# A selective-scan layer with a gated FFN on one Trainium2 core: A dt and B u as float32r halves, the carried state added in PSUM

## The chip, the core and the metric

The kernel runs on one core of a Trainium2 chip. Five engines take part, each with its own instruction queue that it works off in order: PE (TensorE, matrix products; the profile shows its weight loads as a row of their own, PEld), DVE (VectorE), ACT (ScalarE), POOL (GpSimd) and SP (SyncE, which here issues every DMA). Matrix products land in PSUM, which has eight banks of 2 KB per partition; everything else lives in SBUF. The metric is device time in microseconds: 2809.64 us, the median of 3 runs (2807.68 to 2811.33).

## The reference

Two sequences of 1024 tokens with 512 channels go through a selective state-space layer, a layer norm, a gated FFN with 2048 hidden units, and another layer norm. Cut to what matters (all float32; N = 128 states per channel):

```python
xn = rmsnorm(x) * norm_w
xn = xn * sigmoid((xn @ select_proj_w.T + b) * select_gate)
xp = xn @ x_proj_w.T                       # low rank 128, B 128, C 128
delta = softplus(xp[..., :128] @ dt_proj_w.T + dt_proj_b)
A = -exp(A_log)                            # 512 x 128
def step(h, inp):                          # one token
    dt, bt, ct, xt = inp
    h = exp(dt[:, :, None] * A) * h + (dt * xt)[:, :, None] * bt[:, None, :]
    return h, einsum('bdn,bn->bd', h, ct)
y = scan(step, 0, ...)
x = layernorm(x + (y + x * D_param) @ out_proj_w.T)
x = layernorm(x + (silu(x @ w_gate.T) * (x @ w_up.T)) @ w_down.T)
```

## The kernel before

The state of 512 x 128 numbers per token is never stored beyond a few tiles. The 2048 tokens are cut into 64 steps of 32 tokens. A step is worked in two halves of 256 channels, a half in eight rounds of 32 channels, so there are 1024 rounds, numbered k in the loop at line 677 (r is the round within the half, h the half). States lie on the partitions.

In a round, PE makes two things for 32 channels x 32 tokens. One is B u (tile bu, line 700): the 32 tokens are the contraction, the weights are 32 rows of B, the moving operand du is u spread over a one-hot matrix. The other is the argument A dt of the exponential for the next round (tile a, decay_mm, line 409): 32 channels are the contraction, and ddt is dt spread over a one-hot matrix. Each is done in two matmuls of 512 columns (b = 0, 1), each on its own group of 32 array rows; the four matmuls of a round use the four row groups. ACT takes the exponential of a into a_sb (line 416). DVE adds the state carried from the step before to the first token of bu (line 719) and runs one scan of 1024 elements (line 720), which restarts at each channel, since the factor of the first token is kept at zero. The result h goes back to PE for the products with C (y_round, line 433), four column groups at a time, in the rounds that ROUNDS names; y lands in one bank per step, and y_out (line 447) copies it out with ACT and sums it on POOL.

POOL spreads dt and u over the one-hot matrices, one product of 512 elements per round (diag, lines 380 and 390). The carried state needs exp(A dt) of the step's first token: dt of that token is transposed (lines 306 to 316), stored, loaded as cd by all partitions (line 346), multiplied on POOL (line 354), exponentiated on ACT (line 359) and multiplied with the last column of h (line 367).

All else on PE is written as generators that yield: pre (the projections for a block of 128 or 256 tokens), post (the output projection), ffn and silu. Its class Work hands them out: in round r at most PARTS[r] units (and saved credit) of their matmuls follow the two products and the y of that round; their other steps ("E") advance once per round. A pre goes in front of the list, ahead of ffn. B (line 260) and u (line 297) are stored from pre to a DRAM tensor and loaded per step (line 338). FFN weights are fetched through five buffers (line 514), four pieces ahead. All DMAs share SP's one queue, in the order of the program.

PSUM: two buffers of two banks for bu, two banks for a, one for y, one for all other work. So bu of round k waits for the scan of k - 2, and a of round k + 1 for the exponentials of round k.

## Time and profile before

| | |
|---|---|
| median of 3 runs | 2809.64 us (2807.68 to 2811.33) |
| profiled execution: span from first to last instruction | 2803.5 us; its page gives no other time of it |
| mean granted TensorE clock | 0.991 |
| first and last start of a scan | 42.1 and 2728.2 us |
| scan, each, and count | 2287 ns x 1024 |
| DMA | 712 issues on SP, 258.8 MB, mean 92 GB/s |

A row of a group reads: line, engine, operation, output <- inputs, shape, count, then busy time in us and mean ns of one, then idle time of the engine just before and what ended it. A timeline row reads: start in us, length in us, engine, line, operation, output <- inputs, count of merged instructions, and in brackets idle time before it and what ended that. SPq is SP's queue issuing DMAs. An f32 matmul shows as two records. The length of a matmul record includes the way through the array, so records of one batch overlap; the pace is the difference of starts.

### The profile page before, as it was taken

How to read it: one execution, taken by the hardware profiler on the slowest of the kernel's cores; microseconds unless marked ns; L12 is line 12 of the kernel's file. 1: busy time of each engine (PE TensorE's matmuls, PEld its weight loads, DVE VectorE, ACT ScalarE, POOL GpSimd, SP SyncE). 2: the span in 40 equal slices, each digit the busy share in tenths (PEclk: the TensorE clock that was granted, in tenths of full speed). 3: DMA queues.
4: the chain of work that ended last, by engine and by line, in shares of the span. 5: the costliest groups of instructions: out<-in, count | busy, mean ns of one | idle time of the engine just before them, and what ended most of it. 6: DMA issues, size and time to landing. Idle time of an engine off the chain costs nothing.

```text
span 2803.5 us, 59499 instructions
## 1 busy us (share of the span) xinstructions
PE 2688.0 (96%) x23744; PEld 1476.3 (53%) x23744; DVE 2514.2 (90%) x2144; ACT 1549.9 (55%) x3105; POOL 1782.9 (64%) x2016
## 2 busy tenths in 40 slices
PE   6879999999999999999999999999999999999998
PEld 4325545555555554555545555455555555555557
DVE  3999999899999999999999999999999999999980
ACT  4546656645565455655656556565566555555542
POOL 5556666666667576765666657567575666667553
PEclk8999999999999999999999999999999999999999
DMA  2001322423223231233312333132331333332335
GB/s 76 20 27 54 108 80 70 115 82 123 65 83 113 86 125 50 89 103 109 118 56 87 98 115 113 55 93 95 114 95 60 110 97 108 100 109 93 109 99 188
DMA packets 112388, 258.80 MB, mean 92 GB/s; under 512 B 11568, under 2 KB 49456, under 8 KB 112112
## 3 DMA queue, kind: packets, MB, share of 16 engines
q1 hardware_dynamic: 112112, 254.99, 28.3%
q8 instruction: 189, 3.10, 0.5%
q14 instruction: 87, 0.71, 0.1%
HBM read 242.23 MB, written 12.71 MB: 91 GB/s over the span
## 4 chain that ended last, share of the span: by engine, by line
PE 74%; DVE 17%; issue 3%; ACT 3%; POOL 2%; DMA 1%; SPq 0%; DVEq 0%; POOLq 0%; ACTq 0%
PE bu L700 28%; PE gu L540 17%; DVE h L720 15%; PE y L433 12%; PE d L560 8%; PE a L409 3%; ACT a_sb L416 1%; PE sel L187 1%; PE op L481 1%; PE xp L187 1%; DVE bu L719 1%; DMA ub_d<-uT 1%; PE b L251 1%; PE ss L204 1%; SPq L297 0%
## 5 line engine op out<-in xcount | busy, mean ns | idle before, releaser
L720 DVE TENSOR_TENSOR_SCAN h<-a_sb,bu 128x1024 f32<-128x1024 f32 x1024 | 2340.5, 2287 | 154.8 <-PE bu L700 43.5
L416 ACT ACTIVATE a_sb<-a 128x496 f32<-128x496 f32 x2048 | 1089.9, 585 | 1109.0 <-PE a L409 1036.0
L700 PE MATMUL bu<-du,ub 32*128 32x512 f32 x4096 | 1184.3, 643 | 52.8 <-DVE h L720 31.4
L409 PE MATMUL a<-ddt,a_t 32*128 32x512 f32 x4096 | 1209.0, 643 | 2.8 <-ACT t L315 2.8
L380 POOL TENSOR_TENSOR ddt<-dt,hot 128x512 f32<-128x512 f32 x512 | 534.5, 1049 | 193.3 <-PE a L409 193.2
L540 PEld LDWEIGHTS gu<-x1T,w 128*128 128x128 f32 x4096 | 481.2, 192 | 223.7 <-issue 137.3
L390 POOL TENSOR_TENSOR du<-ub,hot 128x512 f32<-128x512 f32 x512 | 535.9, 1051 | 21.8 <-PE a L409 18.5
L540 PE MATMUL gu<-x1T,w 128*128 128x128 f32 x4096 | 535.5, 283 | 6.9 <-ACT t L315 3.5
L433 PE MATMUL y<-h,cz 128*32 128x256 f32 x9208 | 525.1, 361 | 3.0 <-ACT yc L447 1.9
L700 PEld LDWEIGHTS bu<-du,ub 32*128 32x128 f32 x4096 | 329.2, 184 | 352.4 <-issue 190.2
L433 PEld LDWEIGHTS y<-h,cz 128*32 128x32 f32 x9208 | 255.7, 109 | 405.7 <-issue 267.8
L409 PEld LDWEIGHTS a<-ddt,a_t 32*128 32x128 f32 x4096 | 347.9, 184 | 15.9 <-ACT a_sb L416 9.2
L560 PE MATMUL d<-w,hid 128*128 128x256 f32 x1024 | 257.8, 393 | 0.7 <-ACT dt L276 0.3
L578 POOL TENSOR_SCALAR gu<-gu 128x256 f32<-128x256 f32 x128 | 108.4, 847 | 223.4 <-ACT gu L548 222.9
L560 PEld LDWEIGHTS d<-w,hid 128*128 128x128 f32 x1024 | 183.2, 189 | 124.0 <-issue 91.4
L719 DVE TENSOR_TENSOR bu<-bu,cd 128x32 f32<-128x32 f32 x992 | 182.5, 184 | 65.5 <-PE a L409 61.5
L448 POOL TENSOR_TENSOR yc<-yc,pick 128x512 f32<-128x512 f32 x64 | 66.7, 1042 | 195.3 <-ACT yc L447 195.3
L586 POOL TENSOR_TENSOR hid<-gu,e 128x256 f32<-128x256 f32 x128 | 93.1, 727 | 106.1 <-ACT e L584 104.9
L367 POOL TENSOR_TENSOR cd<-cd,h 128x256 f32<-128x256 f32 x124 | 106.4, 858 | 50.2 <-DVE h L720 50.2
L579 POOL TENSOR_TENSOR gu<-gu 128x256 f32<-128x256 f32 x128 | 93.4, 730 | 10.7
L548 ACT COPY gu<-gu 128x512 f32<-128x512 f32 x128 | 75.4, 589 | 33.5 <-PE gu L540 33.4
L325 POOL TENSOR_TENSOR dt<-dt,u 128x512 f32<-128x512 f32 (+1 forms) x36 | 41.4, 1151 | 64.7 <-ACT dt L322 64.7
(86 smaller groups left out, 1243.5 us busy)
## 6 DMA issues: line engine op xcount, KB each, us to landing
w<-in_wgu_s_dram SPq DMA_DIRECT2D x256, 512.0 KB, 3.7
w<-in_wd_s_dram SPq DMA_DIRECT2D x128, 512.0 KB, 3.6
cd<-dt_d SPq DMA_DIRECT2D x62, 256.0 KB, 4.1
ub<-ub_d SPq DMA_DIRECT2D x64, 128.0 KB, 2.0
ub_d<-bt SPq DMA_DIRECT2D x64, 64.0 KB, 1.8
ub_d<-uT SPq DMA_DIRECT2D x64, 64.0 KB, 1.8
zT<-in_x_q_dram SPq DMA_DIRECT2D x16, 256.0 KB, 3.9
x<-in_x_dram SPq DMA_DIRECT2D x16, 256.0 KB, 3.7
```

The lines of the kernel that those rows point to most:

```text
L367: nc.gpsimd.tensor_tensor(cd, cd, last, ALU.mult)
L380: nc.gpsimd.tensor_tensor(ddts[j][:, m, :, :], made[lot_of[st]][0][:, a + m, toks(st)].unsqueeze(1).to_broadcast([P, 16, S]), hot[:, ts(i, ...
L390: nc.gpsimd.tensor_tensor(dus[j][:, m, :, :], uv[:, a + m, :].unsqueeze(2).to_broadcast([P, 16, S]), hot.unsqueeze(1).to_broadcast([P, 16, ...
L409: nc.tensor.matmul(ps, a_t[ts(g, 32), m, :], ddts[k // 4][ts(g, 32), m % 2, :, :], start=True, stop=True,)
L416: nc.scalar.activation(a_sb[:, k % 3, ts(b, 16), 1:], ps[:, :, 1:], AF.Exp, scale=-1.0)
L433: nc.tensor.matmul(ys[st][ts(m, 32), 256 * i + 4 * q0 : 256 * i + 4 * (q0 + nq)], cz[st % 3][:, at : at + 32], hs[h][:, 64 * m + q0 : 64 * ...
L540: nc.tensor.matmul(ps[:, ts(2 * a + b, P)], w[:, a, k, :], x1T[:, k, :], start=(k == 0), stop=(k == NM - 1),)
L560: nc.tensor.matmul(ps[:, 0:HD], hid[:, f, :], w[:, f % 4, :], start=(f == 0), stop=(f == NF - 1),)
L578: nc.gpsimd.tensor_scalar_max(g, g, -80.0)
L700: nc.tensor.matmul(bu[:, ts(b, 16), :], prepared[st][ts(g, 32), 1, :], dus[k // 4][ts(g, 32), m % 2, :, :], start=True, stop=True,)
L719: nc.vector.tensor_tensor(first, first, left[:, at : at + 2, i, :], ALU.add)
L720: nc.vector.tensor_tensor_scan(hs[h][:, ts(r, 32), :].rearrange("p q t -> p (q t)"), a_sb[:, k % 3, :, :].rearrange("p q t -> p (q t)"), b ...
```

## The change

B, u and dt are written as sums of two numbers: a high half rounded to float32r (on ACT, or by a copy to a tile of that type) and the remainder as low half. For A = exp(A_log), laid out by the host in a new order with each row four times, the two halves are built on the chip. The contraction of 32 rows in a row group now holds 8 tokens (for B u) or 8 channels (for A dt) times the four products of high and low halves; sums over 32 tokens become four matmuls of 128 columns (o = 0 to 3), and 16 channels by 32 tokens of A dt become two of 256 columns (e = 0, 1). All have float32r operands.

The carried state is no longer added by DVE. The last column of h is gathered by ACT (gather), transposed on PE into a spare half of the y bank (carry_mm), copied out, multiplied with exp(A dt) of the first token (carry) and added into bu by one more f32 matmul of 16 columns in the same PSUM accumulation (state_mm).

The y bank is now per half; the products of C with h of the half before fall in rounds 1, 2 and 3. h is split into two tiles per half with three buffers in all. The B, u and dt halves go to three DRAM tensors in smaller pieces and are loaded by nine DMAs per step. The transposition of the first dt is gone.

```diff
-ROUNDS = ((), (0, 1, 2), (), (), (3, 4, 5.0), (), (), (5.5, 6, 7))
-PARTS = (4, 0, 3, 3, 0, 3, 3, 0)
+ROUNDS = ((), (0, 1, 2), (3, 4, 5), (6, 7), (), (), (), ())
+PARTS = (3, 0, 0, 0, 3, 4, 4, 3)
...
-    dt0_d = dram.tile([NS, D], FP, name="dt0_d")
-
-    ub_d = dram.tile([NS, 4, S, 2, P], FP, name="ub_d")
+    dt_d = dram.tile([NS, 2, P, NM, S], FP, name="dt_d")
+    u_d = dram.tile([NS, 2, 4, 8, 4, P], FP, name="u_d")
+    b_d = dram.tile([NS, 8, 2, 2, 4, N], FP, name="b_d")
...
+    a_raw = half_pool.tile([P, P, S], FP, tag="h", name="a_raw", bufs=3)
+    a_raw = a_raw.rearrange("p q t -> p (q t)")
+    half_n = 4 * NM * N
+    nc.sync.dma_start(a_raw[:, 0:half_n], a_log_r)
     nc.sync.dma_start(a_t, a_log)
-    nc.sync.dma_start(a_n, a_log_t)
...
-        for t in (a_t, a_n):
-            nc.scalar.activation(t, t, AF.Exp)
+        whole, round_ = a_raw[:, 0:half_n], a_raw[:, half_n:]
+        nc.scalar.activation(whole, whole, AF.Exp)
+        nc.scalar.copy(round_.bitcast(FR), whole)
+        nc.scalar.activation(a_t, a_t, AF.Exp)
+        nc.vector.tensor_scalar_mul(whole, whole, is_lo)
+        nc.vector.scalar_tensor_tensor(
+            a_r.rearrange("p x n -> p (x n)"), round_, sign, whole, ALU.mult, ALU.add
+        )
...
+        nc.scalar.copy(bh, ps[:, 0:n].rearrange("p (j n) -> p j n", n=N))
+        yield "E"
+        bl = bt.bitcast(FR)
+        nc.gpsimd.tensor_tensor(bl, bt, bh, ALU.subtract)
         for st in range(n_s):
-            rows = bt[ts(st % 4, S), st // 4, :]
-            nc.sync.dma_start(
-                ub_d[t0 // S + st, :, :, 1, :].rearrange("g t n -> t g n"),
-                rows.unsqueeze(1).to_broadcast([S, 4, N]),
-            )
+            for c1, piece in enumerate((bh, bl)):
+                first = S * (st % 4)
+                rows = piece.bitcast(FP)[first : first + S, st // 4, :]
+                for o in range(4):
+                    nc.sync.dma_start(
+                        b_d[t0 // S + st, :, c1, :, o, :],
+                        rows[ts(o, 8), :].unsqueeze(1).to_broadcast([8, 2, N]),
+                    )
...
+        for st in range(n_s):
+            for c2, piece in enumerate((dth, dtl)):
+                nc.sync.dma_start(dt_d[t0 // S + st, c2], piece.bitcast(FP)[:, :, ts(st, S)])
...
             for st in range(4):
-                nc.sync.dma_start(
-                    ub_d[t0 // S + 4 * j + st, :, :, 0, :].rearrange("g t q -> t g q"),
-                    t[ts(st, S), :].rearrange("t (g q) -> t g q", g=4),
-                )
+                for c2, piece in enumerate((th, tl)):
+                    rows = piece.bitcast(FP)[ts(st, S), :].rearrange("t (g q) -> t g q", g=4)
+                    for o in range(4):
+                        nc.sync.dma_start(
+                            u_d[t0 // S + 4 * j + st, c2, :, :, o, :].rearrange("g t q -> t g q"),
+                            rows[ts(o, 8), :, :],
+                        )
...
+        for c in range(4):
+            nc.sync.dma_start(
+                dt_r.rearrange("(r c) e s m t -> c r (e s m t)", c=4)[c],
+                dt_d[st, c % 2].rearrange("(r x) m t -> r (x m t)", x=4),
+            )
+            nc.sync.dma_start(
+                u_r.rearrange("(r c) o q -> c r (o q)", c=4)[c],
+                u_d[st, c % 2].rearrange("g t o q -> (g t) (o q)"),
+            )
+        nc.sync.dma_start(
+            b_r.rearrange("p o n -> p (o n)"),
+            b_d[st].rearrange("t a b o n -> (t a b) (o n)").unsqueeze(0).to_broadcast([4, S, 4 * N]),
+        )
...
+    def gather(h):
+
+        lasts[h] = half_pool.tile([P, 2, P], FP, tag="last", name=f"last_{h}", bufs=1)
+        for mm in range(2):
+            nc.scalar.copy(
+                lasts[h][:, mm, :].rearrange("p (q s) -> p s q", s=2),
+                hs[h][mm][:, :, S - 1].rearrange("p (s q) -> p s q", s=2),
+            )
+
+    def carry_mm(h):
+
+        for mm in range(2):
+            nc.tensor.matmul(
+                ys[h][:, 1 - h % 2, ts(mm, N)], lasts[h][:, mm, :], ident,
+                start=True, stop=True, skip_group_check=True,
+            )
+
+    def carry(h):
...
+        nc.scalar.copy(cT.rearrange("p m n -> p (m n)"), ys[h][:, 1 - i, :])
+        yield "E"
+        for mm in range(2):
+            m = 2 * i + mm
+            nc.scalar.activation(a0[:, mm, :], a_t[:, m, :], AF.Exp, scale=nd0[:, m : m + 1])
+        yield "E"
+        nc.gpsimd.tensor_tensor(cT, cT, a0, ALU.mult)
...
-        nc.tensor.matmul(
-            ps, a_t[ts(g, 32), m, :], ddts[k // 4][ts(g, 32), m % 2, :, :],
-            start=True, stop=True,
-        )
+        for e in range(2):
+            nc.tensor.matmul(
+                ps.rearrange("p (d e) t -> p e d t", e=2)[:, e],
+                a_r[ts(g, 32), 4 * m + 2 * e + s, :], ddts[k // 4][ts(g, 32), s, e, :, :],
+                start=True, stop=True, skip_group_check=True,
+            )
...
+    def state_mm(k, b, bu):
+
+        h, mm, s, pair = place(k)
+        st, g = h // 2, 2 * pair + b
+        last = st % NSB == 0
+        for o in range(4):
+            nc.tensor.matmul(
+                bu[:, ts(b, 16), ts(o, 8)], prepared[st][1][ts(g, 32), o, :],
+                dus[k // 4][ts(g, 32), s, o, :, :],
+                start=(o == 0), stop=last and o == 3, skip_group_check=True,
+            )
+        if not last:
+            nc.tensor.matmul(
+                bu[:, ts(b, 16), 0], products[h][ts(g, 32), mm, :],
+                hot[ts(g, 32), :].rearrange("p (e s) -> p s e", s=2)[:, s, :],
+                start=False, stop=True, skip_group_check=True,
+            )
...
+            if h in products:
+                work.finish(carries.pop(h))
...
+        if r == 4 and h:
+            y_out(h - 1)
+            if h - 1 in lasts:
+                carries[h + 1] = work.add(carry(h - 1), front=True)
+        if r == 1 and h and h + 1 < 2 * NS and (h + 1) // 2 % NSB:
+            gather(h - 1)
         work.others()
...
-        if st % NSB:
-            left = carried[st].rearrange("p (b i e) -> p b i e", i=2, e=16)
-            first = bu[:, :, 0].rearrange("p (b e) -> p b e", e=16)
-            at = 4 * m + 2 * pair
-            nc.vector.tensor_tensor(first, first, left[:, at : at + 2, i, :], ALU.add)
...
+            if r == 3 and h - 1 in lasts:
+                carry_mm(h - 1)
```

## The prediction

> **What bounds the kernel now.** I read the page first: shares, the chain that ended last (PE 74%, DVE 17%), and the costliest groups.
>
> ```profile
> PE 2688.0 (96%) x23744; PEld 1476.3 (53%) x23744; DVE 2514.2 (90%) x2144; ACT 1549.9 (55%) x3105; POOL 1782.9 (64%) x2016
> ...
> L720 DVE TENSOR_TENSOR_SCAN h<-a_sb,bu 128x1024 f32<-128x1024 f32 x1024 | 2340.5, 2287 | 154.8 <-PE bu L700 43.5
> ...
> L719 DVE TENSOR_TENSOR bu<-bu,cd 128x32 f32<-128x32 f32 x992 | 182.5, 184 | 65.5 <-PE a L409 61.5
> ```
>
> PE and DVE are both nearly full. The tile view of h puts scan starts from 42.1 to 2728.2: 2686.1 / 1023 = 2.626 us a round, with 42 before the first and 73 after the last (2803.5 - 2730.5). The timeline of the first scans, which have no add before them, and of a stretch in which PE has little else give the DVE's own pace:
>
> ```profile
> 54.68 26.25 DVE L720 TENSOR_TENSOR_SCAN h<-a_sb,bu 128x1024 f32<-128x1024 f32 x12 [2.03 <-PE a L409]
> ...
> 201.32 2.29 DVE L720 TENSOR_TENSOR_SCAN h<-a_sb,bu 128x1024 f32<-128x1024 f32 x1
> 203.52 0.18 DVE L719 TENSOR_TENSOR bu<-bu,cd 128x32 f32<-128x32 f32 x1
> 203.80 2.29 DVE L720 TENSOR_TENSOR_SCAN h<-a_sb,bu 128x1024 f32<-128x1024 f32 x1
> ```
>
> With the add a round is at least 2.48; without it (26.25 - 2.29) / 11 = 2.18. Next, the four matmuls of one round, and what follows them on PE:
>
> ```profile
> 1312.74 0.69 PE L700 MATMUL bu<-du,ub 32*128 32x512 f32 x1
> 1312.75 0.69 PE L409 MATMUL a<-ddt,a_t 32*128 32x512 f32 x1
> 1312.76 0.69 PE L700 MATMUL bu<-du,ub 32*128 32x512 f32 x1
> 1312.76 0.69 PE L409 MATMUL a<-ddt,a_t 32*128 32x512 f32 x1
> ...
> 1313.81 0.38 PE L540 MATMUL gu<-x1T,w 128*128 128x128 f32 x1
> ...
> 1326.32 2.05 PE L540 MATMUL gu<-x1T,w 128*128 128x128 f32 x16
> 1328.30 0.69 PE L700 MATMUL bu<-du,ub 32*128 32x512 f32 x1
> ```
>
> An f32 matmul is two records. The four matmuls use the four row groups and run side by side; the burst lasts 1.07 (1312.74 to 1313.81). Sixteen gu records last 2.05 and eight 1.16 elsewhere, so a record of 128 columns costs 0.111; and from the first of sixteen to the next burst it takes 1.98 (1326.32 to 1328.30), so each switch costs about 0.2.
>
> PE per half (eight rounds): bursts 8 x 1.07 = 8.56; y in three batches, 1.43 (83.10 to 84.53) + 2 x 1.22 (1017.22 to 1018.44) = 3.87; the other work in units of some four 128-column records, 0.446 each. Units by the counts: gu 1024, d 512, op 128, sel 144, xp 72, some 175 more; less about 160 before the first and after the last scan: 1895 / 128 = 14.8 a half = 6.6, and five switches = 1.0. Sum 20.0, or 2.50 a round. The other 0.12 up to 2.626 is rounds where PE has less than the DVE's 2.48.
>
> **The change part by part.**
>
> *DVE.* The 992 adds go. Floor 2.18 a round; PE decides then.
>
> *The burst (B u, A dt, carry).* Per row group, bu now has four float32r matmuls of 128 columns with four weight loads, and the carried state one f32 matmul of 16 columns (two records, two loads); a has two of 256 columns. No row shows float32r. Lower end: half an f32 record per matmul, a quarter of what f32 costs at the same size: 4 x 0.056 + 2 x 0.111 + 0.2 = 0.65. Upper end: each costs what an f32 matmul of its size costs, two records: 4 x 0.223 + 0.22 + 0.2 = 1.31. I take one record of 0.111 per matmul: the operands come already split, so I assume one record instead of two, and that its 128-column weight load keeps the pace of the f32 rows. Six records and a switch: 6 x 0.111 + 0.2 = 0.87; the a groups, two records of at most 0.22 + 0.2, finish inside. Break-even is computed below.
>
> This needs groups to run past each other. The cold bursts speak for it:
>
> ```profile
> 42.60 1.22 PE L409 MATMUL a<-ddt,a_t 32*128 32x512 f32 x1
> 42.61 1.22 PE L700 MATMUL bu<-du,ub 32*128 32x512 f32 x1
> 43.08 1.59 PE L409 MATMUL a<-ddt,a_t 32*128 32x512 f32 x2
> ```
>
> The timeline of PE alone is shown. The bu matmul at 42.61 comes later in the program than both records of a at 42.60, and the second of those starts after it (a cold record of a streams until about 43.4, and the row of two at 43.08 ends at 44.67). One waiting record was passed; up to eleven weight loads and matmuls must be passed now, which no row shows. The Trainium skill ("TensorE: Matmul & The Clock Gate", Part 3, what overlaps and what doesn't) says matmuls start and end strictly in program order, which speaks against the change; these rows contradict it at a depth of one. By it the sum would be that of the serial rival below.
>
> *Other PE work per half.* y without its split matmul: 2 x 1.43 + (2 x 0.427 + 0.2) = 3.91; the transposes of the carried state, 4 records x 0.111 = 0.45; units and switches as before, 7.5 (the nine t0 batches, under 10 us in all, go). Sum 11.9, or 1.49 a round. PE round: 1.49 + 0.87 = 2.36. PE stands 0.18 above the DVE floor where it stood 0.02 above, so I allow half the old unevenness: 2.42. Loop: 1024 x 2.42 = 2478, against 2688.
>
> *ACT.* Out: cd exps 39.5 and t copies 5. In, by nearest rows: gather and exp of the first decay, some 248 each of 128 columns at 0.31 (154); cT copies 124 x 0.37 (46); y_out in two parts (+10); high copies about 20. Net +185, 62% busy. They are issued behind the round's two a_sb exps (1.06), so a round has at worst about 2.8 of ACT; a_sb has three buffers, and PE waits for a bank of a if ACT is late. At most 0.05 a round; it is in the 0.06.
>
> *POOL.* Out: cd products 78.9 + 106.4. In: 124 carry products x 0.73 = 91, the low halves and the negated first dt about 50, constants 2. Net -43. The 1024 one-hot products keep 512 elements (1.05); if writing float32r cost the 1.27 of a product without broadcast, +225 would leave POOL under 80%: nothing. The carry product at round 5 waits for ACT; ddt behind it is due four rounds later. The carry chain itself ends at round 5 and is used at round 0: some 7 us of cover.
>
> *SP.* It issues every DMA here. Its timeline at a block of 256 tokens:
>
> ```profile
> 490.80 3.75 SPq L260 DMA_DIRECT2D ub_d<-bt  x8
> ...
> 495.57 16.28 SPq L514 DMA_DIRECT2D w<-in_wgu_s_dram  x4
> ```
>
> A store costs 0.44 to 0.47 of issue (eight in 3.75; in the start four in 1.78). Per 32 tokens: 8 for B, 2 for dt, 8 for u and 9 loads, 27 issues instead of 4, about 12 us of a 39 us step: bandwidth of the queue suffices. But they come in bunches. Start: 32 + 8 + 32 stores instead of 9 are in series with the first load: +63 x 0.44 = 28, and 1 for POOL's new constants; the other new work (1 MB of a_raw, exps, low halves) lies beside it. First scan at 71. (At the 0.30 of the shortest stores, +19.) In the loop a block of 256 tokens stores 64 for B in one bunch, 28 us, and then 16 (7 us) and twice 32 (14 us each). The weight fetches queue behind. Two f-pairs of weights are in stock at the bunch (495.57 waits for free buffers), worth 5 us of z and 16 units, 23 us; the next arrives after 28 + 0.3 + 3.7 = 32. So about 9 late, less at 0.30 an issue; the later bunches some 3 each. PE stops in order and the bursts with it. I take 10 for each of the six blocks that run beside FFN: 60. Bounds: 0, and 210 (35 each, if every bunch is exposed by half). The Trainium skill ("DMA: Bandwidth & Descriptors", issuing engines are not separate DMA queues) calls issue time usually small beside the transfer. Here 0.44 stands beside 1.8 of landing, and 64 in a row are not small. By the rule this term and most of the +29 would be nothing, 2600.
>
> **Sum.** 71 + 2478 + 60 + 73 = 2682 of span, against 2803.5. The page gives no other time for that execution; the median of the runs is 6.1 above its span, so 2688. A change within 0.2% (about 6 us) could not be told from none.
>
> Break-even: (2803.5 - 71 - 60 - 73) / 1024 = 2.54 a round, less 0.05 and 1.49: a burst of 1.00. Against 1.07 today the forecast has little room.
>
> **Rivals.**
> 1. *float32r at f32's price* for these sizes, or a window too shallow, so that a and the second bu group start late: burst 1.31, round 2.80 + 0.03; 2898 + 204 + 6 = 3108, slower. For: no row shows either. Against: the halves that an f32 matmul's second record seems to be for are already rows of the contraction. It decides from a burst of 1.00.
> 2. *Strict order*: sixteen records one after another, 16 x 0.111 + 0.2 = 1.98, round 3.49: 3574 + 204 + 6 = 3784. Against: 42.61 above.
> 3. *The SP queue*: burst as forecast, but bunches starve FFN's weights by 35 a block: +150, 2838, slower. For: 28 us against 23 of stock. Against: prefetch refills between bunches.
> 4. *Loads half as long*: burst 0.65, PE 2.14, so DVE's 2.18 + 0.1 decides: 2335 + 204 + 6 = 2545.
>
> **How the numbers follow.** Forecast 0.42, rival 4 0.11, rival 1 0.27, rival 2 0.06, rival 3 0.14. Forecast alone: 2600 to 2790. Faster takes forecast and rival 4, less 0.01: 0.52; same 0.03, from the edges of forecast and rival 3; slower 0.45. The range 2560 to 3130 leaves out half of rival 4, rival 2, and the upper part of rival 1: less than 0.2.
>
> **What would show it.** Right: burst to next batch near 0.87, scans 2.18 apart where PE has little, no L719, first scan near 71. Wrong: second bu group's first record about 0.6 after the first group's (strict order); records of 128 columns 0.22 apart (price); FFN's matmuls waiting for w, with SP in stores (queue). ACT over 75% or POOL as releaser of bursts would upset the covers.

## The result, and the profile after

The changed kernel takes 3237.31 us (median of 4 runs, 3234.2 to 3243.81), against 2809.05 us for the kernel before in the same comparison: a ratio of 1.153, 95% interval 1.1515 to 1.1547. The forecast was 2688 us, faster, with a range up to 3130. Sign and range were both wrong.

The page of the changed kernel: its shares, the clock granted to TensorE in forty slices of the span (tenths of full speed, 9 is 90% or more), and the groups that answer to those of before (columns: busy us, mean ns of one | idle us just before and what ended it):

```profile
PE 2875.3 (89%) x31216; PEld 2338.6 (72%) x31216; DVE 2377.6 (74%) x1155; ACT 1731.4 (54%) x3753; POOL 1768.9 (55%) x2011
...
PEclk6679799899988998889997999979989799897898
...
L797 DVE TENSOR_TENSOR_SCAN h<-a_sb,bu 128x1024 f32<-128x1024 f32 x1024 | 2320.7, 2282 | 755.1 <-PE bu L489 671.2
...
L483 PE MATMUL bu<-du,b_r 32*128 32x128 f32 x8192 | 1032.9, 297 | 55.2 <-DVE h L797 36.7
L470 PE MATMUL a<-ddt,a_r 32*128 32x256 f32 x4096 | 853.9, 344 | 35.4 <-POOL ddt L440 28.9
```

DVE fell from 90% to 74%. Its scans now wait 671 us for the last matmul of the burst, the carry at line 489. POOL and ACT are far from full, as forecast. 8192 records for 8192 float32r matmuls of bu, and 4096 for a, say that a float32r matmul is one record. The tile view of h gives the start and the end of the loop:

```profile
L797 DVE TENSOR_TENSOR_SCAN h<-a_sb,bu x1024: 2258/2287/2291, 69.2 to 3158.8; 128x1024 f32<-128x1024 f32 x171
```

First scan at 69.2 us (forecast 71), and 71 us behind the last scan's end (3232.4 less 3161.1; forecast 73). So the whole miss lies in the loop: 3089.6 us between first and last scan start, against 2538 forecast (2478 and 60 of stalls). Three things are in it.

**The burst.** The timeline of PE in one round of the changed kernel (start us, length us, columns of the shape, count of merged records):

```profile
1307.42 0.55 PE L483 MATMUL bu<-du,b_r 32*128 32x128 f32 x3
1307.70 0.38 PE L470 MATMUL a<-ddt,a_r 32*128 32x256 f32 x1
1307.71 0.43 PE L483 MATMUL bu<-du,b_r 32*128 32x128 f32 x3
1307.92 0.23 PE L489 MATMUL bu<-hot,cT 32*128 32x16 f32 x1
1307.93 0.27 PE L470 MATMUL a<-ddt,a_r 32*128 32x256 f32 x1
...
1308.29 0.26 PE L489 MATMUL bu<-hot,cT 32*128 32x16 f32 x1
1308.47 0.71 PE L273 MATMUL b<-xp_w,xT 128*128 128x128 f32 x4
```

1307.42 to 1308.47 is 1.05 us; the median burst is 1.056, against 1.07 before and 0.87 forecast. The first row group's records follow each other by 0.11 us, as forecast (0.16 after the first; medians over the loop). But the first A dt matmul, for a free row group, starts only at 1307.70 and the second B u group at 1307.71, 0.29 us late.

The first step of a sequence has no carried state, so its rounds have the same order without the carry's matmuls. There, in most bursts, all four row groups start within 0.03 us, and this burst lasts 0.60:

```profile
94.88 0.32 PE L483 MATMUL bu<-du,b_r 32*128 32x128 f32 x1
94.89 0.38 PE L470 MATMUL a<-ddt,a_r 32*128 32x256 f32 x1
94.89 0.32 PE L483 MATMUL bu<-du,b_r 32*128 32x128 f32 x1
94.91 0.38 PE L470 MATMUL a<-ddt,a_r 32*128 32x256 f32 x1
```

So PE goes past a row group in which three B u still wait. With the two records of the carry behind them five wait, and the next group starts only when the third B u has started and three are left (B u at 0, 0.164 and 0.275 us, A dt at 0.282, medians).

**The stores.** The waits of PE, then of ACT, in the changed kernel (us in total, times, longest):

```profile
PE gu L621 <- ACT uTh L335: 100.6, 7, 15.6
PE gu L621 <- DMA w<-in_wgu_s_dram: 74.9, 10, 11.3
```

```profile
ACT uT L335 <- DMA u_d<-uT: 101.7, 7, 16.3
```

Rounds (from one scan start to the next) of over 7 us exist 16 times, and exceed 2.7 us each by 215 us in sum (forecast 60, bound 210). Some 75 us are the forecast's mechanism: FFN's matmuls stand and wait for w, which stands on SP behind 64 stores of B:

```profile
1311.24 1.32 SPq L290 DMA_DIRECT2D b_d<-bh  x4
1312.65 1.29 SPq L290 DMA_DIRECT2D b_d<-bt  x4
...
1332.47 1.33 SPq L290 DMA_DIRECT2D b_d<-bt  x4
...
1339.79 0.47 SPq L595 DMA_DIRECT2D w<-in_wgu_s_dram  x1
```

A store issues in 0.3 us, less than the 0.44 taken, and the bunch lasts 22.6 us (1311.24 to 1333.8). The other 100 were not foreseen: the copy of the second 128 tokens of u (line 335) waits up to 16.3 us on ACT until the first 128 tokens' 32 stores have left the one row buffer, and behind it on ACT stand the exps and copies that PE waits for.

**The clock.** The records of TensorE's clock hold full and half clock and nothing between. The mean is 0.890 where it was 0.991, so half clock lasted 2 x 0.110 x 3232 = 711 us (the clock's own records sum to 715; before 51). The forecast had no term for it. Windows of the changed kernel (span, length, then busy us of PE, PEld, DVE, ACT, POOL, with counts, then granted clock, DMA share, GB/s):

```profile
1995.00:1998.00 3.00, 0.61 (x14) 0.51 (x10) 2.90 (x4) 1.44 (x4) 1.11 (x2) 0.94 0.24 79
1998.00:2008.00 10.00, 10.00 (x89) 6.47 (x90) 6.58 (x3) 4.49 (x8) 2.32 (x3) 0.51 0.52 177
2008.00:2015.00 7.00, 6.93 (x85) 5.59 (x82) 5.20 (x3) 6.55 (x16) 2.39 (x4) 1.00 0.42 166
```

A gap of 2.4 us in PE's work, and then ten microseconds in which PE is busy without a pause at half clock. The kernel before, in a stretch with 14 gaps of over 0.8 us (the longest 1.44), keeps its clock:

```profile
120.00:200.00 80.00, 60.12 (x564) 22.77 (x560) 76.12 (x65) 37.03 (x71) 45.24 (x50) 0.98 0.07 20
```

Counted over the loop: before, PE has 35 gaps of 0.8 to 2.4 us, and 6 of them are followed by over 1 us of half clock in the next 6 us. In the changed kernel it has 48, and 47 are. The lengths differ, though: 31 of the 35 are under 1.5 us (4 of them followed by half clock), and 30 of the 48 (29 followed); from 1.5 to 2.4 us it is 2 of 4, and 18 of 18. The changed kernel also has 20 gaps of over 2.4 us, before none.

By rounds, the changed kernel has 864 with the clock held, at 2.706 us on average, and 159 that spend over 0.3 of their length at half clock, 751 us together (4.73 each). Against the forecast's 2.42, the first cost 864 x 0.286 = 247, of which the burst is 864 x 0.186 = 161; the others cost 751 - 159 x 2.42 - 60 = 306. Together 553, and the miss of the time is 549 (3237.3 less 2688).

The 306 are not all the clock's. The 16 rounds of over 7 us are all among the 159, and exceed the 60 that were forecast by 155. The other 143 are 106 us longer than rounds at the same place in the half with the clock held: that, as an estimate, is what the half clock costs beside the stalls.

### The profile page after: what moved, and what is told of

The parts are those of the page before. It is cut to its first block, busy times and chain, and to the rows that moved or that the text cites. A ratio compares the mean times of both kernels' runs of the same rounds, so it can differ in the third digit from the quotient of the medians.

```text
span 3232.4 us, 76245 instructions
## 1 busy us (share of the span) xinstructions
PE 2875.3 (89%) x31216; PEld 2338.6 (72%) x31216; DVE 2377.6 (74%) x1155; ACT 1731.4 (54%) x3753; POOL 1768.9 (55%) x2011
## 5 line engine op out<-in xcount | busy, mean ns | idle before, releaser
L483 PEld LDWEIGHTS bu<-du,b_r 32*128 32x128 f32 x8192 | 883.7, 198 | 323.1 <-issue 202.5
L483 PE MATMUL bu<-du,b_r 32*128 32x128 f32 x8192 | 1032.9, 297 | 55.2 <-DVE h L797 36.7
L470 PE MATMUL a<-ddt,a_r 32*128 32x256 f32 x4096 | 853.9, 344 | 35.4 <-POOL ddt L440 28.9
L440 POOL TENSOR_TENSOR ddt<-dt_r,hot 128x512 fp32r<-128x512 f32 x512 | 533.8, 1051 | 341.7 <-PE bu L489 197.8
L489 PE MATMUL bu<-hot,cT 32*128 32x16 f32 x3968 | 657.8, 251 | 0.0
L470 PEld LDWEIGHTS a<-ddt,a_r 32*128 32x128 f32 x4096 | 627.3, 195 | 39.1 <-POOL ddt L440 29.3
L489 PEld LDWEIGHTS bu<-hot,cT 32*128 32x128 f32 x3968 | 621.9, 199 | 0.0
L449 POOL TENSOR_TENSOR du<-u_r,hot 128x512 fp32r<-128x512 f32 x512 | 556.9, 1103 | 9.6 <-PE bu L483 9.4
L428 POOL TENSOR_TENSOR cT<-cT,a 128x256 f32<-128x256 f32 x124 | 90.5, 730 | 128.8 <-ACT a L426 128.8
L409 PEld LDWEIGHTS y<-ident,last 128*128 128x128 f32 x496 | 65.0, 191 | 51.5 <-issue 51.5
```

The costliest lines, as they stand in the source:

```text
L409: nc.tensor.matmul(ys[h][:, 1 - h % 2, ts(mm, N)], lasts[h][:, mm, :], ident, start=True, stop=True, skip_group_check=True,)
L440: nc.gpsimd.tensor_tensor(ddts[j][:, s, :, :, :], dt_r[:, :, s, m, :].unsqueeze(2).to_broadcast([P, 2, 8, S]), hot8.unsqueeze(1).unsqueeze ...
L449: nc.gpsimd.tensor_tensor(dus[j][:, s, :, :, :], u_r.rearrange("p o (m e s) -> p o m e s", m=NM, s=2)[:, :, m, :, s] .unsqueeze(3).to_broa ...
L470: nc.tensor.matmul(ps.rearrange("p (d e) t -> p e d t", e=2)[:, e], a_r[ts(g, 32), 4 * m + 2 * e + s, :], ddts[k // 4][ts(g, 32), s, e, :, :],
L483: nc.tensor.matmul(bu[:, ts(b, 16), ts(o, 8)], prepared[st][1][ts(g, 32), o, :], dus[k // 4][ts(g, 32), s, o, :, :], start=(o == 0), stop= ...
L489: nc.tensor.matmul(bu[:, ts(b, 16), 0], products[h][ts(g, 32), mm, :], hot[ts(g, 32), :].rearrange("p (e s) -> p s e", s=2)[:, s, :], star ...
```

## The experiments

Each time is compared with the kernel before on the same chip (2808.7 to 2813.5 us). "Half clock" is read from the clock's records of the profiled run. The order, the portions, both, and before without the add were run once each, the last table's two float32r kernels with the carry four times, all others twice.

### Order of the burst, and stores in portions

The theory: PE passes only some three waiting matmuls, so the order of the burst sets its length; and the bunches of stores make the long stalls. Three runs: the order alone, the portions alone, both. The order deals the matmuls of the four row groups out in turn; the portions are extra "E" yields in pre.

```diff
-        for b in range(2):
-            state_mm(k, b, bu)
-            if k + 1 < NG:
-                nxt.append(decay_mm(k + 1, b))
+        states = [state_mm(k, b, bu) for b in range(2)]
+        args = [decay_mm(k + 1, b) for b in range(2)] if k + 1 < NG else []
+        for gens in (states, states, args, args, states, args, states, states):
+            for gen in gens:
+                made_now = next(gen, None)
...
                         rows[ts(o, 8), :].unsqueeze(1).to_broadcast([8, 2, N]),
                     )
+            if c > 1:
+                yield "E"
```

> Only the order of a round's matmuls on TensorE changes: the four row groups take turns instead of one group's five matmuls standing first. Theory (TensorE looks only some three matmuls ahead, so the second group of B u starts 0.29 us late): the burst falls from 1.055 to 6 x 0.11 + 0.2 = 0.87 us, 1024 x 0.19 = 190 us less, about 3050 us. Rival (weight loads or the float32r stream are what fills the burst, whatever the order): burst still 1.05 us, 3237 us.

> The stores of B, dt and u of a block are handed to SP in portions of 4 or 8, one portion per round, instead of 64, 16 and 32 at once; their number stays. Theory (bunches on SP hold up the FFN's weights and the buffer of the transposed u): the stretches of 15 to 20 us without a scan, 214 us in all beyond normal rounds, go, and with them most of the half-clock time that follows them: 3237 - 214 - 60 = about 2960 us. Rival (the stalls are only where PE waits anyway, or the number of issues is what counts): within 50 us of 3237.

> Both of the changes of e1_order and e2_spread. If the two causes are separate the gains add: about 2770 us, burst 0.87 us, no gap between scans above 8 us. If the bunches and the burst hide each other, clearly more than the sum of the parts, 2900 us or more.

Order: 3054.1 us, burst 0.770. Nothing was taken away, and the burst lost 0.286 and the time 183, of 1023 x 0.286 = 293: some rounds are held by DVE now (2.20 us at two places of the half), and the stalls grew from 215 to 251 us, half clock from 715 to some 740. The timeline of PE with the order dealt out:

```profile
1300.70 0.33 PE L483 MATMUL bu<-du,b_r 32*128 32x128 f32 x2
1300.71 0.38 PE L471 MATMUL a<-ddt,a_r 32*128 32x256 f32 x2
1300.86 0.27 PE L483 MATMUL bu<-du,b_r 32*128 32x128 f32 x2
1300.93 0.28 PE L471 MATMUL a<-ddt,a_r 32*128 32x256 f32 x2
1300.97 0.39 PE L483 MATMUL bu<-du,b_r 32*128 32x128 f32 x4
1301.20 0.34 PE L489 MATMUL bu<-hot,cT 32*128 32x16 f32 x4
1301.47 0.71 PE L621 MATMUL gu<-x1T,w 128*128 128x128 f32 x4
```

All four groups start within 0.01 us, where 0.29 lay between the first and the others. No group puts more than two records in a row into the queue before the others have their turn. That the order sets the burst is thereby shown. That the limit is three waiting records of one row group, and not three in all, is read from the orders: without a carry the changed kernel passes three in each of two groups, and the float32 run of the last table starts all four groups within 0.03 us while seven records wait, at most three of one group. No run varied the number alone.

Portions: 3168.2 us, where some 2960 was expected. Of the 16 long rounds two remain, with 51 us of excess, nearly all of it in one round of 48.9 us, which was 20.3 before the portions (the third block's preparation has four steps only). Half clock stayed at 680 us. Both: 2987.5 us, half clock 704. The two gains add (183 and 69, together 250); 2770 was missed because the portions brought 69 us where 277 were expected. So most of the long stalls went (68 us are left in the run of both) and the half clock did not, which the theory of long stalls could not explain.

### Before, without the add on DVE

Line 719 of the kernel before is left out; the state of the step before is then not added.

> The kernel before with the addition of the carried state to bu on VectorE left out (the state is then not carried from step to step; the work that makes it stays). It prices that half of the change by itself. Theory (before, two thirds of the rounds last VectorE's 2.48 us while TensorE has 2.50 on average): the round falls from 2.63 to about 2.53, 2710 us. Rival (TensorE alone sets the round): 2810 us. Floor if TensorE did not matter: 2.18 a round, 2350 us.

2783.9 us, 26 less. The rival's figure of no gain is nearer. The page of this run has PE at

```profile
PE 2714.1 (98%) x23744; PEld 1497.2 (54%) x23744; DVE 2369.0 (85%) x1152; ACT 1549.2 (56%) x3105; POOL 1780.4 (64%) x2016
```

so the add was in PE's shadow almost everywhere: removing it pays little unless PE's round gets shorter too.

### What the clock follows

Four runs on the version with both edits (portions from the fourth block on): that version itself, one with a filling matmul in the rounds that have no unit of other work, one with the same matmul on 32 rows only, one with more filling.

```diff
+        if idle:
+            nc.tensor.matmul(
+                bu[:, 0:16, :].rearrange("p q t -> p (q t)"), ident, out_w[:, 0, :],
+                start=True, stop=True, skip_group_check=True,
+            )
...
+        idle = PARTS[r] and done == 0
```

> The changed kernel with the burst's matmuls dealt out in turn and the stores given in portions, as in the run of both, but the portions only from the fourth block of tokens on (the third block's preparation has too few steps to wait for portions: it left a gap of 49.9 us at round 112). Expected: 2987.5 less about 46, 2940 us; half clock for about 690 us, as before, since the burst streams as little as it did. Rival: the half clock follows from the long gaps alone, and with the last of them gone it falls below 300 us and the time below 2850.

> As the run above, and in front of the burst of each round that has no unit of other TensorE work though it may have one (83 of 1024), one plain float32 matmul of 128x128 by 128x512 into the PSUM bank that the burst then overwrites: it computes nothing that is used, and adds about 0.85 us of full-array streaming to a round of 2.2 to 2.4 us (from the 0.251 us that a float32 record of 256 columns takes in the down projection). Theory (the clock follows the share of the array's column slots that stream): the filled rounds go from a share of 0.10 to 0.45, half clock falls from 690 to 300-450 us, and the time to 2790-2860. Rival (the clock was lost to something else, the filler is only added work): half clock stays within 60 us of the run above, and the time is equal or up to 70 us longer (83 x 0.85).

> As the filled run, but the filling matmul uses 32 rows of the array instead of 128, with the same 512 columns: TensorE is busy just as long, and a quarter of the array streams. Theory of the streaming share: the filled rounds only reach 0.19, and half clock stays within 80 us of the run with no filling (about 690), the time at 2930-2990. Rival (TensorE's busy time sets the clock, whatever part of the array is used): half clock and time fall as in the full-array filling, to within 30 us of that run.

> As the full-array filling, and also a float32 matmul of 256 columns (some 0.43 us) ahead of each burst that follows the rounds 1 and 2 of a half, which hold the y products but no unit of other work; their share goes from about 0.39 to 0.57, and TensorE's work in them from 1.4 to 1.85 us, still under the scan's 2.18. Theory: half clock falls by a further 50-150 us and the time by 20-80 from the other filled run. Rival (those rounds kept their clock anyway, and TensorE is on the path there too): half clock the same, time 0-50 us longer.

| run | time us | ratio to before, 95% | half clock us |
|---|---|---|---|
| both edits | 2958.9 | 1.0495 to 1.0588 | 677 |
| filled, whole array | 2955.5 | 1.0475 to 1.0584 | 581 |
| filled, 32 rows | 2992.7 | 1.0542 to 1.0782 | 725 |
| more filling | 3054.9 | 1.0829 to 1.0938 | 486 |

The whole-array filling takes 96 us of half clock away, and the same columns on 32 rows take none. The mean clock of the second execution of each gives nearly the same: 656 us without filling, 554 with it, 667 on 32 rows, 470 with more. That speaks for the share of the array that streams, and against PE's busy time. But the size fits neither text: 581 lies between the theory's 300 to 450 and the rival's 617 and more. The filling was also expected to bring some 100 us of time and brought none, and more filling costs 96: in the rounds after 1 and 2 PE had less room than the 1.4 of 2.18 us put down for it. Against the filling on 32 rows, which adds as much work, the whole-array one has 144 us less half clock and 37 us less time (the two executions of each lie 9 and 27 us apart): by this estimate half clock costs time, but about a quarter of its length and not half. The waits of PE that the filling leaves are for DVE, w, POOL and ACT, and there no filling stands. In the version itself, with the gap of 49.9 us gone, the time fell by 29 of the 46 us expected, and half clock stayed at 677 us: the longest gaps alone do not bring it.

The same question without added work: float32r alone, put into the kernel before; and plain float32 in place of float32r in the version with both edits.

```diff
-                ddts[j] = half_pool.tile(shape, FP, tag="ddt", name=f"ddt_{j}")
+                ddts[j] = half_pool.tile(shape, FR, tag="ddt", name=f"ddt_{j}")
...
-            ps, a_t[ts(g, 32), m, :], ddts[k // 4][ts(g, 32), m % 2, :, :],
+            ps, a_tr[ts(g, 32), m, :], ddts[k // 4][ts(g, 32), m % 2, :, :],
...
-                bu[:, ts(b, 16), :], prepared[st][ts(g, 32), 1, :],
+                bu[:, ts(b, 16), :], prepared[st].bitcast(FR)[ts(g, 32), 1, :],
```

> The kernel before with one thing of the change alone: the matmuls of the burst take float32r operands (A, dt, B, u rounded once, no low halves: the products are less exact), four of 512 columns, no split, no carry matmuls, no stores added, the same order of work. Expected of the burst: 1.07 to about 0.5 us (two row groups side by side, each 2 x 512 columns at one cycle: 0.43, and a weight load). With the clock held the round would fall from 2.63 to 2.35-2.40 (scan 2.18 and the add), the time to 2500-2560. Theory (a burst that streams a quarter as much lets the clock drop where a gap comes): half clock rises from 51 to 250-600 us and takes back part of the gain: 2560-2750. Rival (the clock loss of the changed kernel comes from its stores and waits, not from float32r): half clock below 100 us, 2500-2560.

> The changed kernel in the order dealt out in turn and with the stores in portions (2958.9 us), its burst's matmuls reading the same tiles as plain float32: same split, same stores, same waits for transfers and POOL, four times the columns' cycles. Expected: burst 0.77 to 1.5-1.8 us (two row groups side by side, each 1024 columns at four cycles: 1.7), median round 3.2-3.6, time 3350-3750. Theory of the streaming share: with the burst streaming 0.85 us of full array again, half clock falls from 677 to below 200 us though the time is longer. Rival (the gaps alone bring the half clock): half clock stays above 400 us.

Float32r alone in before: 2720.4 us (ratio 0.9645 to 0.9701), burst 0.438, half clock 362 us against 51, with no store and no matmul added. The same stretch of the start that kept 0.98 of the clock before, in this run:

```profile
120.00:200.00 80.00, 51.50 (x432) 22.34 (x430) 76.70 (x65) 37.88 (x72) 43.74 (x48) 0.66 0.10 27
```

Plain float32 in the changed order: 3149.4 us (ratio 1.1115 to 1.1282), half clock 236 against 677 with the same stores, loads and order, though the run is 190 us longer. 236 lies between the theory's 200 and the rival's 400, and the time is below the 3350 to 3750 expected. The burst is 1.220, not 1.5 to 1.8: the expectation let two row groups run side by side, and there are four. The same program shows two things in its two number types. With the longer burst PE has fewer gaps of 0.8 to 2.4 us, 46 against 89. And the short ones lose the clock less often: of those under 1.5 us 11 of 34 are followed by half clock in float32, 52 of 63 in float32r. From 1.5 us on there is no such difference: 11 of 12, and 23 of 26. With float32r alone it is 40 of 109 and 40 of 51. So gaps bring the half clock on, the short ones mostly where the burst streams little. How much of the 441 us is owed to fewer gaps, and how much to the streaming, was not parted. The granted clock of the plain float32 run in forty slices, from its page, to be held against the changed kernel's row above:

```profile
PEclk6989989999999999999999999999999999999998
```

The Trainium skill ("TensorE: Matmul & The Clock Gate", Part 1, what's actually happening) says that a free-running window of some 3.4 us decides, by how busy PE has been. The stretches of half clock here are indeed 3.4 us or multiples of it; but 1998 to 2008 shows PE 10.00 of 10 us busy at 0.51, so busy in the profile's sense is not what decides. An estimate of the streaming itself: a float32 record of 256 columns in the down projection takes 0.216 us from start to start, 0.84 ns a column; a float32r record is taken at half of that (assumed), and each record is weighted with the part of the array's rows and columns that it uses. By it, the 3.4-us windows of the changed kernel before a fall have at most some 0.37 of the array streaming, median 0.19, and those that keep full clock a median of about 0.6 (before: about 0.8). The lowest of those are no higher than the highest before a fall, and before, windows of 0.26 kept full clock, so no threshold follows.

### Loads of w from ACT, and no carry

> As the 2958.9 us kernel, with the feed-forward weights' loads issued from ScalarE's queue in place of SyncE's, so that they no longer stand behind the stores and the row loads. Theory: TensorE's waits for w (59 us in 14 gaps over 1.2 us) go, with the half clock that follows them (92 us, of which half is lost): 2850-2910. Rival (an issue costs ScalarE as much as SyncE, 0.35 us x 384 = 134 us, and it lies between the exps of a round): no faster than 2950, up to 3080.

```diff
-                nc.sync.dma_start(pieces[i], sources[i])
+                nc.scalar.dma_start(pieces[i], sources[i])
```

2953.7 us (ratio 1.037 to 1.0635): no difference that can be told from 2958.9. The largest of PE's waits in this run shows what came instead:

```profile
PE a L477 <- ACT a_sb L502: 56.5, 46, 5.6
```

PE's wait for w, 44.5 us with the loads on SP, is gone from the head of the list, and the burst's wait for the exponentials, 22.0 us there, is 56.5. The loads are now issued on the queue of the exps, as the rival said, and there was no gain.

> As the 2958.9 us kernel, with the carried state left out altogether (no gather, no transpose, no exp of the carry, no carry matmul in the burst; the state starts at zero in every half, so the output lacks the carried part). Burst expected 0.77 to 0.55 (two matmuls of two records fewer). If TensorE sets the rounds with units (five of eight): 5/8 x 1023 x 0.22 = 140 us less, 2800-2840. Rival (what TensorE gains turns into gaps at half clock): 2880-2950, half clock over 720 us.

```diff
-        last = st % NSB == 0
+        last = True
...
-        if r == 1 and h and h + 1 < 2 * NS and (h + 1) // 2 % NSB:
-            gather(h - 1)
```

2765.0 us (0.9799 to 0.9865), 194 less than with the carry, where 140 was expected, and level with before or a little under it. Burst 0.592, so 0.178 less a round, 182 us if every round had it. Half clock is 609 us. So with order and portions mended, the carry costs more than the 149 us that are left between 2958.9 and before.

### Which part costs: the change without its split

The changed kernel, with one A dt and one B u matmul of 512 columns per row group and before's stores and loads, first with float32r operands rounded once, then in plain float32, then with float32r and another order of the burst.

```diff
-        for e in range(2):
-            nc.tensor.matmul(
-                ps.rearrange("p (d e) t -> p e d t", e=2)[:, e],
-                a_r[ts(g, 32), 4 * m + 2 * e + s, :], ddts[k // 4][ts(g, 32), s, e, :, :],
-                start=True, stop=True, skip_group_check=True,
-            )
+        nc.tensor.matmul(
+            ps, a_r[ts(g, 32), m, :], ddts[k // 4][ts(g, 32), s, :, :],
+            start=True, stop=True, skip_group_check=True,
+        )
...
-        for o in range(4):
-            nc.tensor.matmul(
-                bu[:, ts(b, 16), ts(o, 8)], prepared[st][1][ts(g, 32), o, :],
-                dus[k // 4][ts(g, 32), s, o, :, :],
-                start=(o == 0), stop=last and o == 3, skip_group_check=True,
-            )
+        nc.tensor.matmul(
+            bu[:, ts(b, 16), :], prepared[st].bitcast(FR)[ts(g, 32), 1, :],
+            dus[k // 4][ts(g, 32), s, :, :],
+            start=True, stop=last, skip_group_check=True,
+        )
```

> The changed kernel without its split: float32r operands rounded once (no low halves, the products are less exact), one A dt matmul and one B u matmul of 512 columns per row group as before, before's stores and one row load a step, and all the rest of the change: the order of channels, the carried state transposed and added in PSUM, C h early. If the split (its 12 more matmuls a round, its stores and row loads) is what costs, burst 0.6-0.7 us (0.44 in the run of before with float32r, and two small matmuls of two records), rounds with units 2.4-2.6, the others at the scan's 2.18, half clock 300-500 us: 2560-2720, below the 2720 of before with float32r alone. Rival (the carry's chain or the early C h costs as well: gaps of TensorE stay): 2750-2900.

> As the run above with plain float32 throughout, so the carry in PSUM and the early C h alone: the kernel before with only the second and third part of the change. Burst expected 1.07 plus 0.1 to 0.2 for the carry, and no add on VectorE. Theory (TensorE set the rounds of before, so that the add removed is worth 1% and the carry's matmuls cost more than that): 2850-3000, half clock below 100 us. Rival (the carry's matmuls fit into idle time, the add's removal is a gain): 2700-2800.

> As the first of these three, with the burst's matmuls in the order both B u, both A dt, both carries, so that neither carry stands in front of a group that is free. Theory (TensorE passes only about three waiting matmuls): burst 0.1-0.15 us shorter than in the first, in the five rounds of eight with units on the path: 30-90 us less time. Rival (six matmuls are within the look-ahead, or VectorE sets the rounds by now): within 15 us of the first.

| kernel | time us | ratio to before, 95% | burst us | half clock us |
|---|---|---|---|---|
| before | 2809.7 | 1 | 1.071 | 51 |
| carry in PSUM and early C h alone, float32 | 3065.5 | 1.0891 to 1.0935 | 1.198 | 182 |
| float32r alone | 2720.4 | 0.9645 to 0.9701 | 0.438 | 362 |
| float32r, carry in PSUM, early C h | 2641.1 | 0.9381 to 0.9417 | 0.566 | 380 |
| the same, carries last in the burst | 2616.0 | 0.9300 to 0.9330 | 0.557 | 370 |
| the change (with the split) | 3237.3 | 1.1515 to 1.1547 | 1.056 | 715 |

The split, with the stores and loads that it needs, is the part that costs most: without it the same kernel is at 2641, with it at 3237, and still at 2959 with the order and the portions mended. The carry and the early C h alone, in float32, cost 256 us, more than the 190 at most that was expected: PE is busy 2942.6 us in that run, 254 more than before, and the median round is 2.63 to 3.21 us by its place in the half. 1023 x 0.127 = 130 us are the longer burst, 58 the transposes (128 halves at the forecast's 0.45); the remaining 68 were not parted. Half clock is 182 us there, 131 more than before, where less than 100 was expected: part of it comes without float32r (20 of 33 gaps are followed by it). With float32r the same part gains 79 us (2720.4 to 2641.1), because there DVE set the round. The scans and adds of float32r alone:

```profile
L722 DVE TENSOR_TENSOR_SCAN h<-a_sb,bu 128x1024 f32<-128x1024 f32 x1024 | 2339.1, 2287 | 144.4 <-PE bu L702 39.3 <-DVE bu L721 2.3 <-ACT a_sb L418 0.9
L721 DVE TENSOR_TENSOR bu<-bu,cd 128x32 f32<-128x32 f32 x992 | 176.7, 178 | 15.1 <-PE a L411 13.5 <-PE bu L702 1.5
```

The scan waits 39 us for PE in all, and the median round is 2.48 at every place in the half. That is the DVE's pace with the add, so there half clock costs little: a round at half clock lasts 2.63 on average, one with the clock held 2.53. Without the add, five of eight rounds come down to 2.18 to 2.20.

The order with the carries last gains 25 us of the 30 to 90 expected; its burst is only 0.009 shorter, and the gain shows at the first of the three long rounds of a half (2.48 to 2.34). Neither text holds the time, but the burst is the rival's: no row group has more than two records waiting here, and in both orders the four groups start within 0.03 us. The limit read from the changed kernel is not reached. At 2616.0 us this is the fastest kernel of the study, 6.9% under before. It rounds each operand once, so its products are less exact than those of both kernels; it is not a replacement for the change where that matters.

## Why the prediction was wrong

- **Start, tail, record, covers: right.** 69.2 against 71, 71 against 73, one record per float32r matmul at 0.11 us, POOL and ACT busy 55% and 54%.
- **The burst: the failed step.** "This needs groups to run past each other" was taken from a cold row that showed one waiting record passed, and stretched to eleven weight loads and matmuls. The runs show that PE passes three waiting records of a row group and not the five of this order: 0.87 became 1.056. That is above the forecast's own break-even of 1.00, so by its own sum this step turns the sign (1024 x 0.186 = 190 us more, 2878). The forecast's own rows at 1312.74 to 1312.76 could have told more than the cold ones: the fourth group starts there while a second record waits in each of three others. The order dealt out, with the same matmuls, gives 0.770, under the forecast: the sum of records held, and its order was not looked at. But with that burst the kernel is at 3054.1, still slower than before, so the steps below would have turned the sign too.
- **The rivals.** Rival 1 had two conditions. float32r at float32's price fell; the window too shallow, "so that a and the second bu group start late", is what happened, at 1.056 instead of 1.31. The forecast gave the two together 0.27. Its time of 3108 had neither the 215 us of stalls nor the clock in it. Strict order (rival 2, 1.98) was further off, on the other side. The Trainium skill ("TensorE: Matmul & The Clock Gate", Part 3, the mechanism) speaks of a reorder window 64 deep. If that is read as matmuls passing that many, the 0.29 us of lateness in the burst's timeline contradict it.
- **The mean round: mis-sized.** The forecast added 0.06 for unevenness to a mean PE round. With the burst at 0.770 its formula gives 1.49 + 0.77 + 0.06 = 2.32, and the rounds with the clock held took 2.508 on average: by their place in the half they last from 2.20 to 2.75 (medians), since rounds with little for PE stop at DVE's 2.18 and cannot pay for those with four units.
- **The clock: a missing term.** Some 660 us more at half clock, put above at 106 us of time beside the stalls. The forecast counted the streaming that float32r takes away only as time saved. The short gaps are mostly waits that were there before (PE's waits for h are 31 us before and 37 after); they became dear as the burst no longer holds the clock. The long ones, for w and for the copy of u, are new. The runs at plain float32 and at float32r part clearly (236 against 677, 51 against 362), so float32r operands bring the larger part; 236 and 182 us in float32 with the carry, against 51, show that they do not bring all. That it is the share of the array is supported by the fillings, two executions each, and not shown.
- **SP's bunches: right in kind, mis-sized.** 60 was taken, 215 measured, where the bound was 210. The issue was cheaper (0.3 for 0.44); the row buffer of u behind its own stores was not seen, and makes 101 of the 175 us of PE's two waits.
- **DVE: right in its floor, and without effect.** 2.18 is reached, in the runs where PE's round is shorter. "PE decides then" was already nearly so before: 26 us.

## What to carry to other kernels

Before matmuls on several row groups are split into more and smaller ones, write down the order in which they enter the queue, and count what waits in each group: the sum of their times holds only if the groups alternate, since TensorE passed three waiting records of a group here and not five. When a cheaper number type takes streaming away from TensorE, ask of every gap that was free until now whether the clock still holds behind it, and price the rounds at half clock by what bounds them: little where VectorE does (2.63 against 2.53 us). And price parts of a change in both worlds: the carry in PSUM costs 256 us where TensorE sets the round and gains 79 where VectorE does.

## What the runs showed of the hardware

- TensorE goes on past matmuls that wait in one row group to those of others: past three waiting records of a group with some 0.03 us of delay (the changed kernel's rounds without a carry), past five not (0.29 us, its other rounds). With the groups dealt out it is 0.01.
- A float32r matmul is one record, a float32 one two; a burst of four 512-column matmuls on the four row groups takes 0.438 us against 1.07.
- TensorE can be busy 10.00 of 10 us at a granted clock of 0.51. 47 of 48 gaps of 0.8 to 2.4 us were followed by half clock in the changed kernel, 6 of 35 before. In one program, of gaps of 0.8 to 1.5 us 52 of 63 were with float32r operands and 11 of 34 with float32; of longer ones nearly all with both.
- Filling idle rounds with whole-array work lowered half clock by 96 us and saved no time; on 32 rows it lowered nothing.
